# Where the third quarter's turns of layer 0's attention stand in the queues: step by step behind the first half's chain instead of behind the router

## The chip, the cores and the metric

The kernel runs on one core of a Trainium2 chip. A core has a matrix engine (PE), a vector engine (DVE), an engine for activation functions (ACT), a general engine (POOL), and a queue engine that starts transfers (SP). Each works through its own instructions in order; they wait for each other by semaphores. The metric is device time in microseconds (us): the median of three runs, which before the change is 1929.3 (1927.78 to 1932.83).

## The reference

An activation x of 4 rows, 1024 steps and 128 features goes through four layers. Each layer has a mixing part ("attn") and a part by token ("ffn"), and after each part a layer norm of the sum: x = norm(x + part(x)). What matters here are layers 0 and 1:

```python
# layer 0, attn: a short convolution gives a value, a gate and a score; then, for M = 4 angles,
phi = x5 * theta
re_m = poly * cos(phi);  im_m = poly * sin(phi)
num_re, num_im, den = split(cumsum(concat([p_w * re_m, p_w * im_m, p_w]), axis=1))
re = num_re / max(den, 1e-4);  im = num_im / max(den, 1e-4)
rs = rsqrt(mean of the squares over one head + 1e-5)
y = re * rs * norm_scale[:16] @ W_re + im * rs * norm_scale[16:] @ W_im
out = (y * silu(gate)) @ out_proj_w
# layer 0, ffn: x in blocks of 32 rounded to a 6 bit grid, times a weight treated likewise, plus a bias
# layer 1, attn: a complex recurrence h_t = a * h_{t-1} + B u_t; y_t = Re(C h_t)
# layer 1, ffn: a router picks 4 of 16 experts for each token; their outputs are added with weights
```

Both attention parts run along the steps, so a quarter of the steps needs the carried sums of the quarter ahead of it. The router and the experts go token by token.

## The kernel before, in words

The 1024 steps are cut into four quarters of 256. A tile of a quarter has 128 partitions (features) and 4 rows x 256 steps, so 1024 elements. The first two quarters are the first half, "a": they go ahead through layer 0 and layer 1 up to layer 1's experts, and the third and fourth follow beside that.

**Layer 0's attention** is `l0_attn` (L378 on). For each quarter, `prepare(q)` projects value, gate and score (16 matmuls of 512 columns and 16 of 256), and makes the weight `pq` and the running sum `den`. Then come four *turns*, one for each angle m. A turn takes, on ACT, two rows for `k` (L447, L448), then sine, Abs and sine again (L451, L452, L454); on DVE one row for `k` (L449), and for each of the parts im and re a product with `pq` (L456), the carry from the quarter before (L366) and a scan over the steps (`l0_scan`, L367); then on ACT a square of the scan's result (L460) and a copy of its last step (L369), and on PE two matmuls into `yv` and four for the sum of squares. The *close* of a quarter (L473 to L489) takes the root of that sum (L474, L475), spreads it over the heads on PE, scales the gate, projects, adds to x and normalizes (`norm`, L189 on: statistics on DVE at L196 and L197, the root on ACT at L200, an offset on DVE at L208, eight normalizing rows on ACT at L211).

**The first half's chain** goes on with `l0_ffn` (L530 on; quantizing rows on DVE, L499 to L519, into `xd`; the add to x is L563), `l1_attn` (L648 on; products at L669, scans at L673, carries at L683 to L689, a product on POOL at L691, the add to x at L700), and `l1_route`: logits on PE, a sigmoid on ACT (L785), then only DVE rows from L787 until it has written, at L1302, the positions at which each token's row goes into the lists of its experts. `spread` (L1373 on) then starts 64 indirect DMAs on POOL (L1327), one for 128 tokens and one of their four choices. The experts' first inputs are loaded by SP when all 64 have landed (`gathered`, L1392).

**What sets the order.** The kernel's functions are generators: each `yield (t,)` ends a step and gives its length as planned by hand. `run` takes a generator to its end. `mix(main, side, pace, drain)` alternates: after each step of the main one it takes steps of the side one until their lengths times `pace` make up for it. Each instruction of a side step gets a dependency, without a semaphore, on the last main instruction on its engine ("queued behind"). Then a scheduler orders each engine's instructions by times that it assumes and by these dependencies; in what is not bound by them it may draw an instruction forward past others. So the order in which the functions are called is not yet the order in a queue. `press(side, ready)` takes steps of a side generator until a condition holds.

Before the change, `all` runs `l0_attn((0, 1))`, which also prepares the third quarter, then the chain, the router, and after it `l0_attn((2, 3))` mixed with the spread:

```python
self.run(self.l0_attn((0, 1)))
...
self.run(self.l0_ffn((0, 1)))
self.run(self.l1_attn((0, 1)))
self.run(self.l1_route(a))
self.run(self.mix(self.l0_attn((2, 3)), self.spread("l1", a, K1)))
```

Buffers that matter: the projections' `z` lie in a pool of two in PSUM ("l0z"), which `l0_attn` opens and closes itself; `ms`, the sum of squares, is one of two buffers of the pool `side`, which the router uses as well.

Of the kernel before, what the change touches and what calls it, by code (L numbers as in the profile page):

```python
# [20 lines left out]
P = 128  # L21
# [53 lines left out]
class Kernel:  # L75
# [302 lines left out]
    def l0_attn(self, qs):  # L378

        nc, tc, col = self.nc, self.tc, self.col
        ts, tt = nc.vector.tensor_scalar, nc.vector.tensor_tensor
        x, x0T, taps, cb = self.x, self.x0T, self.taps, self.col["conv_b"]
        with ExitStack() as ctx:
            bp, tp, psy = self.l0_bp, self.l0_tp, self.l0_psy
            psz = self.pool(ctx, "l0z", 2, space=PSUM)
            pss = self.side

            def prepare(q):  # L390
                z2 = self.tile(pss, [P, BLK], "s")[:, :TQ]
                for k in range(CK):
                    for b in range(B):
                        self.mm(
                            z2[32 * b : 32 * b + 32, :], taps[:, k, 2 * P :], x0T[:, q, b, k : k + TQ],
                            k == 0, k == CK - 1,
                        )
                pw = self.tile(bp, [P, TQ], "pw")
                ts(pw, z2, cb[:, 2:3], col["score"], ALU.add, ALU.mult)
                ts(pw, pw, -20.0, 20.0, ALU.max, ALU.min)  # L400
                nc.scalar.activation(pw, pw, AF.Exp)
                tt(pw, pw, self.tw[:, q, :], ALU.mult)

                def project(ch):
                    z = self.tile(psz, [P, QC], "z")
                    for h in range(2):
                        for k in range(CK):
                            self.mm(
                                z[:, h * BLK : (h + 1) * BLK].rearrange("p (b t) -> p b t", b=2),
                                taps[:, k, ch * P : (ch + 1) * P],  # L410
                                x0T[:, q, 2 * h : 2 * h + 2, k : k + TQ],
                                k == 0,
                                k == CK - 1,
                            )
                    return z

                z = project(0)
                xv = self.tile(bp, [P, QC], "xv")
                nc.scalar.activation(xv, z, AF.Identity, bias=cb[:, 0:1])
                z = project(1)  # L420
                gate = self.tile(bp, [P, QC], "gate")
                nc.scalar.activation(gate, z, AF.Silu, bias=cb[:, 1:2])
                pwx = self.l0_spread(psz, pw)

                pq = self.tile(bp, [P, QC], "pq")
                ts(pq, xv, self.nw2, self.dw[:, 1:2], ALU.mult, ALU.add)
                tt(pq, pq, xv, ALU.mult)
                nc.vector.scalar_tensor_tensor(pq, pq, self.dw[:, 0:1], pwx, ALU.add, ALU.mult)
                den = self.tile(bp, [P, QC], "den", bufs=1)
                self.l0_scan(den, pwx, 2 * MF, q)  # L430
                ts(den, den, 1e-4, None, ALU.max)
                nc.scalar.activation(den, den, AF.Square)
                return xv, gate, den, pq

            made = self.l0_made
            if not made:
                made[qs[0]] = prepare(qs[0])
                yield (20.0,)
            for q in qs:
                xv, gate, den, pq = made.pop(q)  # L440
                ms = self.tile(pss, [P, BLK], "s")[:, :TQ]
                self.l0_by_head(ms, self.headd, den, True, False)
                yv = self.tile(psy, [P, QC], "yv")
                for m in range(MF):

                    k = self.tile(tp, [P, QC], "k")
                    nc.scalar.activation(k, xv, AF.Identity, scale=self.turn[:, m : m + 1], bias=self.rnd)  # L447
                    nc.scalar.activation(k, k, AF.Identity, bias=self.drop)  # L448
                    nc.vector.scalar_tensor_tensor(k, xv, self.turn[:, m : m + 1], k, ALU.mult, ALU.subtract)  # L449
                    im = self.tile(tp, [P, QC], "im")  # L450
                    nc.scalar.activation(im, k, AF.Sin, scale=2.0 * PI_IN)  # L451
                    nc.scalar.activation(k, k, AF.Abs)  # L452
                    re = self.tile(tp, [P, QC], "re")
                    nc.scalar.activation(re, k, AF.Sin, scale=-2.0 * PI_IN, bias=self.halfpi)  # L454
                    for part, v in ((1, im), (0, re)):
                        tt(v, v, pq, ALU.mult)  # L456
                        s = self.tile(tp, [P, QC], "s", bufs=3)
                        self.l0_scan(s, v, 2 * m + part, q)
                        sq = self.tile(tp, [P, QC], "sq")
                        nc.scalar.activation(sq, s, AF.Square)  # L460
                        first, last = m == 0 and part == 1, m == MF - 1 and part == 0
                        for h in range(2):
                            c = slice(h * BLK, (h + 1) * BLK)
                            self.mm(yv[:, c], self.wbd[:, part * MF + m, :], s[:, c], first, last)
                        self.l0_by_head(ms, self.head, sq, False, last)
                        yield (5.0,)
                    if m == 0 and q + 1 in qs:
                        made[q + 1] = prepare(q + 1)
                        yield (10.0,)
                if q == 1:  # L470
                    self.l0_weight()
                    made[q + 1] = prepare(q + 1)
                rs = self.tile(bp, [P, TQ], "rs")  # L473
                nc.scalar.activation(rs, ms, AF.Sqrt, scale=1.0 / (2.0 * HC * MF))  # L474
                nc.vector.reciprocal(rs, rs)  # L475
                rsx = self.l0_spread(psz, rs)
                for g in range(2):
                    c = slice(g * BLK, (g + 1) * BLK)
                    tt(gate[:, c], rsx[:, c], gate[:, c], ALU.mult)
                    tt(gate[:, c], yv[:, c], gate[:, c], ALU.mult)  # L480
                for g in range(2):
                    po = self.tile(pss, [P, 4, D], "s")
                    for k in range(4):
                        t = g * 4 + k
                        self.mm(po[:, k, :], gate[:, t * P : (t + 1) * P], self.w_out)
                    t0 = q * QT + g * 4
                    tt(x[:, t0 : t0 + 4, :], po, x[:, t0 : t0 + 4, :], ALU.add)
                self.norm(self.quarter(q), by="act", on_act=True)
                yield (10.0,)  # L489
# [1399 lines left out]
    def at_once(self, gen):  # L1889

        for _ in gen:
            yield (0.0,)

    def served(self, gen, *others):

        others = list(others)
        while True:
            while others and others[0][0]():
                yield from others.pop(0)[1]
            got = next(gen, None)  # L1900
            if got is None and not others:
                return
            yield got or (1.0,)
# [53 lines left out]
    def all(self):  # L1957
# [4 lines left out]
        with ExitStack() as ctx:  # L1962
            lgp = self.pool(ctx, "l2lg")
            self.l2_lg = self.tile(lgp, [P, NT, E2], "lg")
            with ExitStack() as early:

                self.l0_setup(early)
                self.l2_wr = self.load(lgp, self.ins["l2_wr"])
                with ExitStack() as room:
                    self.l0_room(room)  # L1970
                    self.run(self.l0_attn((0, 1)))
                    self.l1_setup()
                    self.zero_lists("l1")
                    self.run(self.l0_ffn((0, 1)))
                    self.run(self.l1_attn((0, 1)))

                    self.run(self.l1_route(a))
                    self.run(self.mix(self.l0_attn((2, 3)), self.spread("l1", a, K1)))
                self.zero_lists("l2", "l3")
                with ExitStack() as c2:  # L1980
                    wall = self.l1_wall(c2)
                    yp = self.pool(c2, "l1ya", 5, right=True)
                    side = self.chain(self.l2_norms(), self.l0_ffn((2, 3), True), self.l1_attn((2, 3), True))
                    self.run(self.mix(self.chain(self.l1_shared(a, self.l1_sw), self.l1_experts(a, wall)), side, 2.0, False))
                    self.run(self.mix(self.abreast(self.l2_weights(), side), self.l1_close(a, yp)))
# [237 lines left out]
```

## Time and profile before

| | before |
|---|---|
| median of three runs | 1929.3 us |
| the profiled execution | 1937.33 us |
| its span in the profile | 1935.5 us |
| PE busy | 1541.5 us (80%) |
| DVE busy | 1199.2 us (62%) |
| ACT busy | 900.6 us (47%) |
| POOL busy | 690.3 us (36%) |

The profile is of one execution; its times in the text are us from the start of its span. L12 is line 12 of the kernel before. "Busy" leaves out waiting. An arrow in brackets tells what ended the idle time ahead of an instruction. An instruction is written with the tile that it writes, an arrow, and the tiles that it reads. The granted clock is the share of full speed that PE had. In the changed kernel the lines stand up to three further down in most places.

### The profile page before, as it was taken

The page shows a single profiled execution, that of the slowest core. Times are in us where ns is not written, and L with a number is a line of the kernel's source. Part 1 is how long each engine was busy: PE and PEld are TensorE (multiplying, and loading weights), DVE is VectorE, ACT ScalarE, POOL GpSimd, SP SyncE. Part 2 cuts the span into 40 slices and gives each one's busy share as a digit, 9 for nine tenths or more (in the row PEclk, how much of TensorE's full clock was granted, in tenths as well). Part 3 has the DMA queues.
Part 4 walks back from the last instruction along what each step waited for, and adds up shares of the span by engine and source line. Part 5 has one row for each costly group of instructions (what it writes and reads, how often), then busy time and mean ns, then how long its engine had stood idle before and what let it go on. Part 6 is the DMA issues. An engine that isn't in the chain of part 4 may idle for free. (4 is left out here: it accounts for less than half of the span.)

```text
span 1935.5 us, 27095 instructions
## 1 busy us (share of the span) xinstructions
PE 1541.5 (80%) x9025; PEld 920.8 (48%) x9025; DVE 1199.2 (62%) x3491; ACT 900.6 (47%) x1349; POOL 690.3 (36%) x670
## 2 busy tenths in 40 slices
PE   7885677597847887989977878798798998999850
PEld 3332433385423345856632232333355757768650
DVE  8998698465766664635564565546442446866383
ACT  5876265243324554423336756564532236644330
POOL 2000148604630660265443000030536430567775
PEclk9897688798978998999988988898988999989985
DMA  9990002244430113632241000000452213425452
GB/s 297 288 288 10 1 17 86 87 126 133 159 129 18 60 63 129 183 96 73 78 137 32 1 1 1 2 23 1 159 213 83 66 28 93 141 68 167 122 147 61
DMA packets 215530, 187.10 MB, mean 97 GB/s; under 512 B 16528, under 2 KB 194064, under 8 KB 214864
## 3 DMA queue, kind: packets, MB, share of 16 engines
q1 hardware_dynamic: 194672, 142.29, 23.6%
q0 software_dynamic: 20704, 42.86, 7.3%
q8 instruction: 84, 1.38, 0.3%
q14 instruction: 70, 0.57, 0.1%
HBM read 88.49 MB, written 96.60 MB: 96 GB/s over the span
## 5 line engine op out<-in xcount | busy, mean ns | idle before, releaser
L1081 ACT ACTIVATE pr<-sc 128x1024 f32<-128x1024 f32 x288 | 279.4, 1021 | 175.2 <-PE sc L161 174.8
L161 PE MATMUL sc<-qm,kT 32*128 32x512 f32 (+3 forms) x1536 | 197.7, 559 | 16.7 <-ACT pr L1081 16.7
L161 PE MATMUL s<-pr,va 128*32 128x512 f32 (+3 forms) x1536 | 167.5, 532 | 19.0 <-DVE x L1019 10.2
L161 PE MATMUL gu<-ld,xgT 128*128 x640 | 165.1, 400 | 10.2 <-DVE hg L1812 5.9
L1087 DVE TENSOR_TENSOR pr<-pr,ld 128x512 f32<-128x512 f32 (+1 forms) x160 | 91.7, 581 | 105.6 <-ACT pr L1081 105.4
L161 PE MATMUL gu<-wall,xgT 128*128 x304 | 148.2, 612 | 2.0 <-ACT xgT L171 2.0
L161 PEld LDWEIGHTS sc<-qm,kT 32*128 32x128 f32 x1536 | 83.7, 194 | 112.4 <-issue 61.1
L161 PEld LDWEIGHTS gu<-ld,xgT 128*128 128x128 f32 x640 | 119.5, 198 | 34.7 <-DVE hg L1812 6.1
L1812 DVE TENSOR_TENSOR hg<-sg,gu 128x256 f32<-128x256 f32 x160 | 66.0, 417 | 92.0 <-ACT sg L1811 91.6
L173 DVE COPY hT<-tp 128x512 f32<-128x512 f32 x118 | 80.9, 686 | 66.2 <-PE tp L169 66.2
L1567 ACT ACTIVATE sg<-gu 128x512 f32<-128x512 f32 x76 | 45.4, 597 | 144.7 <-PE gu L161 143.6
L1811 ACT ACTIVATE sg<-gu 128x256 f32<-128x256 f32 x160 | 61.3, 385 | 107.7 <-PE gu L161 79.8
L171 ACT COPY xgT<-tp 128x512 f32<-128x512 f32 x99 | 58.0, 586 | 99.9 <-PE tp L169 99.8
L1327 POOL DMA_INDIRECT l1ra<-x,posl1a x64 | 79.8, 1246 | 61.3 <-DVE peq L1321 42.0
L1327 POOL DMA_INDIRECT l1rr<-x,posl1r x64 | 65.4, 1022 | 100.9 <-DVE posl1r L1302 70.8
L169 PEld LDWEIGHTS tp<-ld,hg 128*128 128x128 f32 x624 | 77.4, 141 | 49.0 <-issue 32.5
L1569 DVE TENSOR_TENSOR hg<-sg,gu 128x512 f32<-128x512 f32 x76 | 51.8, 682 | 78.9 <-ACT sg L1567 78.8
L1327 POOL DMA_INDIRECT l2rm<-x,posl2m x16 | 15.7, 983 | 236.8 <-DVE peq L1320 230.1
L169 PE MATMUL tp<-ld,hg 128*128 128x128 f32 x624 | 96.4, 275 | 3.7 <-DVE hg L1812 2.0
L1327 POOL DMA_INDIRECT l3ra<-x,posl3a x64 | 63.7, 996 | 93.3 <-DVE usedl3a L1315 51.0
L161 PEld LDWEIGHTS s<-pr,va 128*32 128x32 f32 x1536 | 37.1, 113 | 122.6 <-issue 78.4
L161 PE MATMUL yp<-ld,hT 128*128 x640 | 86.1, 276 | 2.3 <-DVE mv L197 1.5
(447 smaller groups left out, 3439.1 us busy)
## 6 DMA issues: line engine op xcount, KB each, us to landing
wall<-wall SPq DMA_DIRECT2D x16, 768.0 KB, 7.8
l3ra<-zero SPq DMA_DIRECT2D x1, 6144.0 KB, 25.5
ld<-in_l_w SPq DMA_DIRECT2D x2, 3072.0 KB, 10.6
wall<-we SPq DMA_DIRECT2D x24, 256.0 KB, 2.1
ld<-in_l_w SPq DMA_DIRECT2D x1, 6144.0 KB, 20.6
l1ra<-zero SPq DMA_DIRECT2D x1, 5120.0 KB, 19.6
l1rr<-zero SPq DMA_DIRECT2D x1, 5120.0 KB, 23.1
xg<-l3ra SPq DMA_DIRECT2D x20, 256.0 KB, 2.9
```

Of the source, the lines that this page charges most:

```text
L161: return self.nc.tensor.matmul(out, lhsT, rhs, start=start, stop=stop)
L169: nc.tensor.transpose(pt[:, k * P : (k + 1) * P], s, self.ident)
L171: nc.scalar.copy(dst, pt[:, : n * P])
L173: nc.vector.tensor_copy(dst, pt[:, : n * P])
L1081: nc.scalar.activation(pr, sc[h], AF.Exp)
L1087: nc.vector.tensor_tensor(d, d, cst["tril"].unsqueeze(1).unsqueeze(1).to_broadcast([P, 2, n, P]), ALU.mult)
L1327: ins = self.nc.gpsimd.indirect_dma_start(**kw)
L1567: nc.scalar.activation(sg, gu[:, 0, :], AF.Silu)
L1569: nc.vector.tensor_tensor(h, sg, gu[:, 1, :], ALU.mult)
L1811: nc.scalar.activation(sg, pg[:, :, 0, :], AF.Silu)
L1812: nc.vector.tensor_tensor(h[:, 2 * c : 2 * c + 2, :], sg, pg[:, :, 1, :], ALU.mult)
```

## The change

`l0_attn((2, 3))` is no longer called as a whole behind the router. Its first part, the four turns of the third quarter, is mixed into `l0_ffn` and `l1_attn` of the first half, eight steps of 5.0 at a pace of 2.7 against a chain of 108 planned units. Each step's instructions are queued behind the chain's latest on their engine. When all four turns are out, the generator notes "l0 turned" and is left where it is. Behind the router it goes on: the fourth quarter's preparation, the third's close, then the fourth quarter, mixed with the spread; here it is the main generator and the spread the side one, as before. The fourth quarter's preparation, which was written behind the third quarter's first turn, is now behind its last. The pool "l0z" is opened outside: once around the first two quarters, and again behind the router.

```diff
@@ l0_attn
-            psz = self.pool(ctx, "l0z", 2, space=PSUM)
...
-                    z = self.tile(psz, [P, QC], "z")
+                    z = self.tile(self.l0_psz, [P, QC], "z")
...
-                    if m == 0 and q + 1 in qs:
+                    if m == 0 and q != 2 and q + 1 in qs:
                         made[q + 1] = prepare(q + 1)
                         yield (10.0,)
                 if q == 1:
                     self.l0_weight()
+                if q == 2:
+                    self.listed.add("l0 turned")
+                    yield (0.1,)
+                if q in (1, 2):
                     made[q + 1] = prepare(q + 1)
...
+    def until(self, gen, ready):
+
+        while not ready() and (got := next(gen, None)):
+            yield got
@@ all
-                    self.run(self.l0_attn((0, 1)))
+                    with ExitStack() as z:
+                        self.l0_psz = self.pool(z, "l0z", 2, space=PSUM)
+                        self.run(self.l0_attn((0, 1)))
                     self.l1_setup()
                     self.zero_lists("l1")
-                    self.run(self.l0_ffn((0, 1)))
-                    self.run(self.l1_attn((0, 1)))
-
+                    more = self.l0_attn((2, 3))
+                    turned = lambda: "l0 turned" in self.listed
+                    self.run(self.mix(
+                        self.chain(self.l0_ffn((0, 1)), self.l1_attn((0, 1))), self.until(more, turned), 2.7, False
+                    ))
                     self.run(self.l1_route(a))
-                    self.run(self.mix(self.l0_attn((2, 3)), self.spread("l1", a, K1)))
+                    self.press(more, turned)
+                    self.l0_psz = self.pool(room, "l0z", 2, space=PSUM)
+                    self.run(self.mix(more, self.spread("l1", a, K1)))
```

More of the change, by code (lines that the diff above doesn't have):

```diff
@@ L422, in prepare @@
                 nc.scalar.activation(gate, z, AF.Silu, bias=cb[:, 1:2])
-                pwx = self.l0_spread(psz, pw)
+                pwx = self.l0_spread(self.l0_psz, pw)
                 pq = self.tile(bp, [P, QC], "pq")
@@ L475, in l0_attn @@
                 nc.vector.reciprocal(rs, rs)
-                rsx = self.l0_spread(psz, rs)
+                rsx = self.l0_spread(self.l0_psz, rs)
                 for g in range(2):
```

## The prediction, made before the changed kernel ran

> **What bounds the kernel at this place.** I read first the busy time of the engines in four stretches of the span (columns: length, busy us and instructions of PE, weight loads, DVE, ACT and POOL, granted clock, DMA share, GB/s), cut where the first half's chain changes its character.
>
> ```profile
> 140.00:194.35 54.35, 33.35 (x111) 17.92 (x112) 47.28 (x99) 33.39 (x57) 0.00 (x0) 0.78 0.13 37
> 194.35:242.01 47.66, 29.24 (x121) 22.03 (x121) 30.33 (x71) 10.75 (x24) 6.67 (x2) 0.68 0.00 1
> 242.01:265.71 23.70, 19.14 (x64) 8.24 (x66) 21.68 (x124) 12.13 (x11) 0.00 (x0) 0.86 0.00 1
> 265.71:364.69 98.98, 69.10 (x336) 35.12 (x328) 70.38 (x117) 54.98 (x71) 79.77 (x64) 0.86 0.21 78
> ```
>
> They are the quantized layer, layer 1's scan, the router, and the spread of the first half's rows (64 indirect DMAs on POOL). No engine is full in all four, so the bound is a chain. Second, POOL in order of time (start, duration, instruction, idle before it):
>
> ```profile
> 265.71 1.12 POOL L1327 DMA_INDIRECT l1ra<-x,posl1a  x1 [42.05 <-DVE peq L1321]
> 267.14 1.97 POOL L1327 DMA_INDIRECT l1ra<-x,posl1a  x1 [0.31 <-issue]
> 269.42 2.18 POOL L1327 DMA_INDIRECT l1ra<-x,posl1a  x1 [0.30 <-issue]
> 271.90 3.53 POOL L1327 DMA_INDIRECT l1ra<-x,posl1a  x1 [0.30 <-issue]
> ...
> 323.31 0.96 POOL L1327 DMA_INDIRECT l1ra<-x,posl1a  x1 [0.30 <-issue]
> ...
> 363.73 0.96 POOL L1327 DMA_INDIRECT l1ra<-x,posl1a  x1 [0.30 <-issue]
> ```
>
> POOL waits for nothing from the first to the last. Undisturbed, one takes 0.96 and the next starts 0.30 later: 64 x 1.26 = 81 us; the spread took 99. Third, DVE in order of time around it:
>
> ```profile
> 266.04 2.28 DVE L367 TENSOR_TENSOR_SCAN s<-keep,re 128x1024 f32<-128x1024 f32 x1
> 268.55 2.28 DVE L367 TENSOR_TENSOR_SCAN s<-keep,im 128x1024 f32<-128x1024 f32 x1
> 272.38 2.28 DVE L367 TENSOR_TENSOR_SCAN s<-keep,re 128x1024 f32<-128x1024 f32 x1
> ...
> 349.55 0.35 DVE L502 RECIPROCAL qri<-qsc 128x32 f32<-128x32 f32 x1
> 366.67 0.69 DVE L508 TENSOR_SCALAR qt<-qt 128x1024 int32<-128x1024 int32 x1 [16.77 <-POOL qt L505]
> ```
>
> From 350 to 367 DVE has nothing to do, and PE idles 17.11 us before 370.76: the experts' inputs wait until all 64 DMAs have landed, and DVE waits for the POOL product queued behind the spread. So the end of the spread sets what follows, one for one. Its end is the start of the spread, which is when DVE writes the positions (L1302), plus its length. The changed kernel must bring one of the two forward. Fourth, the first half's chain on DVE ahead of the router:
>
> ```profile
> 194.35 2.48 DVE L669 TENSOR_TENSOR b<-pu,wi 128x512 f32<-128x512 f32 x4 [5.85 <-PE pu L161]
> ...
> 209.69 0.69 DVE L700 TENSOR_TENSOR x<-po,x 128x512 f32<-128x512 f32 x1 [2.49 <-PE po L161]
> ...
> 227.53 0.69 DVE L700 TENSOR_TENSOR x<-po,x 128x512 f32<-128x512 f32 x1 [3.85 <-PE po L161]
> ...
> 242.01 0.42 DVE L787 TENSOR_TENSOR s<-sc,rows 128x256 f32<-128x256 f32 x1 [9.19 <-ACT sc L785]
> ```
>
> There are gaps to fill: with two smaller ones some 23 us. Which of the third quarter's work fills them already? None: between 194 and 265 DVE runs none of it. But of its four turns, all but three scans have run by 188, between the rows of the quantized layer.
>
> **What moves.** The written order says that the turns come behind the router; the scheduler had already drawn them forward. The instructions' order in the changed program, set against the old, shows on DVE: exactly three scans cross the router (2.28 us each, those of the third fence). On ACT six squares cross it, on PE the sums of squares and the last matmuls of three scans. The other moves are within the chain: turns 1 to 3, which stood in the quantized layer, now stand one by one in it, in layer 1's two quarters and just ahead of the router. POOL's and SP's queues keep their order; no DMA is added. The order of what follows the spread is the same. ACT gets two more loads of its function tables (98 against 96).
>
> So the price is how much of some 16 us of DVE work (two k rows at 1.2, four products at 1.15, four scans at 2.2, each from start to start) lies ahead of a chain row instead of in a gap. I walked the new order row by row, each row starting when its engine and its inputs are free, with the durations of the same rows of the trace. Four parts up to the router:
>
> 1. To layer 1's first scan: **-3.3**. Ahead of the first quantized tile (xd, L519) stood four scans, two k rows and three products, 14.9; now one scan, one product and one k row, 4.5. That is -10.4, less 1.3 for a product now ahead of the second quarter's close: -9.1. Behind it stood 4.6 of turns; now two products, two scans and a k row, 7.9: +3.3. A square (1.05) and a sine table swapped for the root's (1.28) stand ahead of the norm on ACT: with their waits +2.5.
> 2. To the root of layer 1's first norm: **+7.9**. A product and a scan stand ahead of the carry rows that release POOL's product (L691): +3.4. The second quarter's two scans now come ahead of the first add to x (L700), which waited for PE only 2.49: +3.6. A product and a scan stand ahead of the statistics, +3.3, and one scan of the chain no longer stands among them, -2.3.
> 3. To the root of the second norm: **+2.7**. The statistics are ready about as late as part 2 leaves them, but ACT is in turn 3: two k rows, sine table, two sines, one Abs, root table, some 8.2 in all, and ends 2.6 after them.
> 4. To the router's first row (L787): **+4.1**. A product and a scan stand ahead of the norm's offset, 3.4, of which 0.8 is covered by the wait for the root; a second scan and two squares break into ACT's eight normalizing rows, +2.2; the logits on PE, at a higher clock, -0.7.
>
> Sum +11.4. The gaps were waits of the chain for a round through ACT, PE or POOL, and in-order rows of 3.4 at their end push the round that follows. The router itself (23.7) keeps its rows: 0.
>
> **The spread: -3.8.** Its first four DMAs took 1.12 + 1.97 + 2.18 + 3.53 = 8.80, undisturbed 3.84: 4.96 too long. The second, third and fourth end 0.77 to 0.80 after a scan of the third fence ends. With the scans gone, the weights' products (L1320 and L1321, 0.42 each) and two k rows still stand there; I keep 1.2 for them. All the fourth quarter's scans and products stay in the spread. Bounds: 0, if these rows delay as much, and -4.96.
> The Trainium skill weighs in here: by "SBUF — State Buffer", section "Who interferes with whom", a DVE instruction with two SBUF inputs contends with GpSimd's reads alone, and it infers that descriptor generation needs the write interface, so that such rows don't stall a DMA. The rows above speak against that inference; by it the saving would be 0 and the sum +11.4.
>
> **PE's clock** in the new order isn't in the trace. In layer 1's stretch it was granted 0.68; 32 matmul records of L161 (po<-l1c,g) took 6.76 and 6.18, against 1.95 for 16 of po<-wT,xdT. The turns' matmuls between them may keep the clock up. The first product no longer decides (part 2); the second and the logits' second half (3.59) at full clock give -3.1 and -1.8 at most. Slower rows of this kind than these the trace doesn't have, so the other end is 0. I keep 0 to -4.9, and I take the -0.7 of part 4, nearer to the rows as they are.
>
> **Sum:** +11.4 - 3.8 = +7.6 us. Against the profiled execution (span 1935.5, time 1937.3) that is a span of 1943.1; against the median of the three runs, 1929.3, it is **1936.9**, +0.4%.
>
> **Rivals.**
> - *Slower still*: the spread keeps its length and turn 3 holds ACT for its full 8.2 behind the copies of xT. +11.4 and up to 3 more: 1941 to 1944. For it: each scan displaced is replaced by another of the fourth quarter sooner; against: those rows' count in the spread is unchanged. 0.10.
> - *No change*: half of parts 2 to 4 (14.7) falls into the gaps because rows end a little earlier than in my walk: +4 - 3.8 = 0, 1929. For it: 23 us of gaps; against: the scans stand directly ahead of the rows that wait. 0.18.
> - *Faster*: the gaps swallow the turns. PE's warmer clock brings the chain's rounds forward by 4.9, DVE's rows lie inside the waits, and of part 1's -3.3 most is kept; the router starts some 3 earlier and the spread is 3.8 shorter: -7, 1922. With a spread 3.8 shorter it turns to a gain where the positions (L1302), at 264.7 now, are written before 268.5, and to one of 0.3% before 262.7. 0.10.
> - *It does nothing*, as the scheduler had done it already. Three scans and the squares do move; counted with no change.
>
> **Chances.** The forecast has 0.62, with a range of its own of 1935.2 to 1941. What a measurement of this kernel can tell from no change is about 0.3%, 5.8 us. Slower by more: 0.62 + 0.10 = 0.72; within: 0.18; faster: 0.10. The range 1926 to 1944 leaves out most of the faster case and the end of the slowest; the costs' bounds (+11.4 with no saving; +11.4 - 4.96 - 4.2 = +2.2) lie inside.
>
> **What would show it.** Right: the first DMA of the spread starts near 277 instead of 265.71, the spread lasts about 95, no scan of the third quarter is left in it, and the experts' first row of DVE (L1812 before) comes some 8 later; on DVE, scans directly ahead of the statistics of layer 1. Wrong: the first DMA starts before 270, which breaks parts 2 to 4; a spread of 99 breaks the saving; a PE clock above 0.85 between the quantized layer and the router breaks the clock's term; another order of rows behind the spread, or a stage after it that changes its length, breaks "one for one".

## The result, and the profile after

The changed kernel takes **1944.2 us** (median of 8 runs, 1938.4 to 1945.5) against 1929.9 (8 runs, 1926.5 to 1935.6): a ratio of 1.0061, 95% interval 1.0046 to 1.0076, or +11.8 us (8.9 to 14.7); the medians themselves differ by 14.3. A ratio here and below is taken from the executions that lie within 1.5% of the fastest one of their kernel. The forecast was 1936.9, +7.6: the sign is right and the size too small; the median lies 0.2 over the end of the range of 1926 to 1944.

The profiled execution of the changed kernel has a span of 1939.1 and a time of 1941.13. That is only 3.8 over the profiled execution of before (1937.33). This execution of before was 6.8 slower than the mean of its 8 timed runs (1930.6), and that of after 1.6 faster than the mean of its own (1942.7); 3.8 + 6.8 + 1.6 makes the 12.2 between the means. So the two traces can be compared place by place, but their ends understate the loss.

First the engines' busy time in the four stretches, now cut at the changed kernel's own boundaries: its first row of layer 1's products, of the router, of the spread, and POOL's product behind the spread (columns as before: length, busy us and instructions of PE, weight loads, DVE, ACT and POOL, granted clock, DMA share, GB/s).

```profile
140.00:192.54 52.54, 35.41 (x144) 18.17 (x144) 39.20 (x88) 29.88 (x53) 0.00 (x0) 0.76 0.13 37
192.54:254.73 62.19, 38.24 (x171) 21.01 (x170) 47.67 (x86) 31.22 (x47) 6.67 (x2) 0.73 0.00 1
254.73:277.19 22.46, 16.43 (x62) 7.07 (x64) 21.63 (x124) 15.72 (x15) 0.00 (x1) 0.86 0.00 0
277.19:369.85 92.66, 63.34 (x252) 33.86 (x244) 62.42 (x113) 41.91 (x55) 73.44 (x64) 0.79 0.22 83
```

The lengths were 54.35, 47.66, 23.70 and 98.98. The quantized layer is 1.8 shorter and the router 1.2; the spread is 6.3 shorter; layer 1's scan is 14.5 longer, with 17.3 more on DVE and 20.5 more on ACT: the turns stand there now. PE's clock in it is 0.73, up from 0.68.

POOL in order of time, the start of the spread, its last DMA and the product behind it:

```profile
277.19 1.12 POOL L1330 DMA_INDIRECT l1ra<-x,posl1a  x1 [50.70 <-DVE peq L1324]
278.62 1.10 POOL L1330 DMA_INDIRECT l1ra<-x,posl1a  x1 [0.30 <-issue]
280.02 1.39 POOL L1330 DMA_INDIRECT l1ra<-x,posl1a  x1 [0.30 <-issue]
281.72 0.96 POOL L1330 DMA_INDIRECT l1ra<-x,posl1a  x1 [0.30 <-issue]
...
368.88 0.95 POOL L1330 DMA_INDIRECT l1ra<-x,posl1a  x1 [0.30 <-issue]
369.85 1.93 POOL L508 TENSOR_TENSOR qt<-x,qri 128x1024 f32<-128x1024 f32 x1
```

The first DMA starts 11.5 later than before (265.71), the first four take 4.57 instead of 8.80, and the product behind the spread, which stood at 364.71, starts 5.1 later. It follows the last DMA without a wait, as before.

DVE in order of time, at two places of the chain:

```profile
169.10 1.22 DVE L522 TENSOR_TENSOR xd<-qt,qsc 128x1024 f32<-128x1024 f32 x1
...
171.70 2.29 DVE L367 TENSOR_TENSOR_SCAN s<-keep,im 128x1024 f32<-128x1024 f32 x1
179.51 0.69 DVE L566 TENSOR_TENSOR x<-po,x 128x512 f32<-128x512 f32 x1 [5.53 <-PE po L161]
...
215.76 0.67 DVE L703 TENSOR_TENSOR x<-po,x 128x512 f32<-128x512 f32 x1
216.34 1.22 DVE L455 TENSOR_TENSOR re<-re,pq 128x1024 f32<-128x1024 f32 x1
217.47 0.69 DVE L703 TENSOR_TENSOR x<-po,x 128x512 f32<-128x512 f32 x1
...
218.14 0.29 DVE L196 BATCH_NORM_STATS2 bn<-x 128x6 f32<-128x128 f32 x1
218.35 2.28 DVE L367 TENSOR_TENSOR_SCAN s<-keep,re 128x1024 f32<-128x1024 f32 x1
```

The lower rows are what the forecast named: a product (L455) between the two adds to x (L703), and a scan behind the first row of the statistics. The upper rows are something that it did not name: the quantized tile xd starts at 169.10, and before the add to x DVE waits 5.53 for PE. PE in order of time says why:

```profile
170.47 1.94 PE L169 MATMUL tp<-ld,xd 128*128 128x128 f32 x8 [9.12 <-DVE xd L522]
172.24 1.23 PE L161 MATMUL po<-wT,xdT 128*128 128x128 f32 x4
174.04 3.78 PE L161 MATMUL yv<-s,wbd 128*128 128x512 f32 x4 [0.58 <-DVE s L367]
177.75 1.08 PE L161 MATMUL s<-sq,ld 128*32 128x256 f32 x8
178.76 1.60 PE L161 MATMUL po<-wT,xdT 128*128 128x128 f32 x12
```

The chain's sixteen matmuls into po are cut in two by the turn's matmuls, which had to wait for the turn's scan (171.70 to 173.99) and then took 3.78 and 1.08. In the kernel before, the sixteen run in one piece, and the add comes 5.8 behind xd (DVE and PE, two views of the same stretch):

```profile
177.65 1.20 DVE L519 TENSOR_TENSOR xd<-qt,qsc 128x1024 f32<-128x1024 f32 x1
183.44 1.28 DVE L563 TENSOR_TENSOR x<-po,x 128x512 f32<-128x512 f32 x2
```

```profile
180.75 1.95 PE L161 MATMUL po<-wT,xdT 128*128 128x128 f32 x16
```

ACT in the changed kernel, at turn 3 and the second norm:

```profile
238.44 1.15 ACT L453 ACTIVATE re<-k,halfpi 128x1024 f32<-128x1024 f32 x1
239.61 1.28 ACT L200 ACT_TABLE_LOAD   x1
240.90 0.30 ACT L200 ACTIVATE rstd<-mv,eps 128x8 f32<-128x8 f32 x1
```

The turn's last sine and the table load behind it end at 240.89 and set the root; DVE's last row of the statistics, itself behind a product of the turn, ends at 239.9.

### The profile page after: what moved, and what is told of

Read it like the earlier page. It is cut to its first block, busy times and chain, and to the rows that moved or that the text cites. A ratio compares the mean times of both kernels' runs of the same rounds, so it can differ in the third digit from the quotient of the medians.

```text
span 1939.1 us, 27097 instructions
## 1 busy us (share of the span) xinstructions
PE 1537.0 (79%) x9025; PEld 921.8 (48%) x9025; DVE 1200.9 (62%) x3491; ACT 902.9 (47%) x1351; POOL 689.9 (36%) x670
## 5 line engine op out<-in xcount | busy, mean ns | idle before, releaser
L161 PE MATMUL s<-pr,va 128*32 128x512 f32 (+3 forms) x1536 | 163.8, 522 | 20.5 <-DVE x L1022 9.7
L161 PE MATMUL yv<-s,wbd 128*128 128x512 f32 x128 | 77.6, 734 | 39.0 <-DVE s L367 35.6
L1330 POOL DMA_INDIRECT l1rr<-x,posl1r x64 | 65.9, 1030 | 100.0 <-DVE posl1r L1305 72.4
L1330 POOL DMA_INDIRECT l1ra<-x,posl1a x64 | 73.4, 1148 | 69.9 <-DVE peq L1324 50.7
## 6 DMA issues: line engine op xcount, KB each, us to landing
ld<-in_l_w SPq DMA_DIRECT2D x2, 3072.0 KB, 10.8
```

What stands on the lines that cost most here:

```text
L161: return self.nc.tensor.matmul(out, lhsT, rhs, start=start, stop=stop)
L1330: ins = self.nc.gpsimd.indirect_dma_start(**kw)
```

## The experiments

**Theories.** A: the turns cost what stands of them ahead of a row of the chain, the spread is long because DMAs wait for DVE rows, and its end hands the sum on. B: the loss comes from what was put behind the router (the third quarter's close, the fourth's preparation, the pool). C: a stage behind the spread has become longer by itself. D: DVE rows do not hold up the DMAs.

**The chips.** The twelve runs were made on three other chips of the same kind, on which the kernel before takes 2240 to 2244 us instead of 1930. The start and the end of the spread agree with the first trace (the kernel before starts it at 265.60 instead of 265.71 and ends it at 364.46 instead of 364.69), so they can be carried over; rows ahead of it differ between traces of one kernel by up to 3 us (layer 1's first scan stands at 196.75 and 198.69). The one repeated trace of before is from the first of the three chips, and places of all twelve are set against it. From 335 on the third and fourth quarters' own chain differs, and behind the spread everything does: the stretches of over 2 us in which PE, DVE and ACT all stand still come to 161 us in the kernel before, against 34 in the first trace. Times are compared only with runs of before on the same chip. They vary by 2 to 3% there, so most intervals are near 1% wide, and a ratio depends on which executions it is taken from: by the medians of all executions the two runs of psum_scan are 0.2% and 0.7% slower than before instead of the 1.4% and 1.0% in the table, in_ffn 0.7% instead of 0.0%, held_back 2.2% and held_psum 2.6%.

All runs in one table; us from the trace, the ratio against before with its 95% interval. "End" is the end of the last of the 64 DMAs, "product" the start of POOL's row behind it.

| kernel | first DMA | length | end | product | ratio |
|---|---|---|---|---|---|
| before, first trace | 265.71 | 98.97 | 364.69 | 364.71 | |
| after, first trace | 277.19 | 92.65 | 369.83 | 369.85 | 1.0061 (1.0046 to 1.0076) |
| before_again | 265.60 | 98.86 | 364.46 | 381.50 | one execution |
| after_again | 276.42 | 92.73 | 369.15 | 386.00 | one execution |
| after_second | 276.48 | 93.93 | 370.41 | 388.07 | 1.0024 (0.9981 to 1.0067) |
| pools_only | 264.87 | 97.36 | 362.24 | 377.88 | 1.0011 (0.9972 to 1.0050) |
| pools_only_second | 265.62 | 98.50 | 364.12 | 381.00 | 1.0018 (0.9981 to 1.0055) |
| in_ffn | 273.38 | 93.60 | 366.98 | 384.99 | 1.0004 (0.9962 to 1.0046) |
| psum_scan | 263.63 | 89.84 | 353.47 | 392.02 | 1.0143 (1.0075 to 1.0211) |
| psum_scan_second | 265.09 | 87.69 | 352.78 | 404.52 | 1.0099 (1.0056 to 1.0143) |
| psum_scan_after | 277.52 | 85.79 | 363.31 | 378.19 | 1.0081 (1.0036 to 1.0126) |
| psum_scan_after_second | 276.49 | 85.84 | 362.33 | 385.58 | 1.0003 (0.9946 to 1.0059) |
| held_back | 246.04 | 94.17 | 340.21 | 442.66 | 1.0180 (1.0091 to 1.0268) |
| held_psum | 246.30 | 86.08 | 332.37 | 447.04 | 1.0357 (1.0293 to 1.0421) |

**1. Both kernels again** (no edit).

> The kernel before, unchanged, for a second profile. Theory A (the change's price is the rows of the turns that stand ahead of rows of the first half's chain; the end of the spread sets what follows one for one): the first DMA of the spread starts within 1 us of 265.71 and the POOL product behind the spread within 1 us of 364.71, as in the first profile; what differs between two executions of one kernel lies behind 1100. Theory C (the stages behind the spread differ between the two kernels, beyond what the spread hands on): the stages behind 1100 lie within 1.5 us of those of the first profile.

> The changed kernel, unchanged, for a second profile. Theory A: first DMA within 1 us of 277.19, POOL product behind the spread within 1 us of 369.85, and behind 1100 an offset to the kernel before that differs from the first pair's (+5.9 at 1108, +0.9 at 1384) by as much as two profiles of one kernel do. Theory C: a stage behind the spread is longer than before by some 6 us in this profile too, at the place where it is in the timed runs.

> The changed kernel again, with a profile and five rounds, because the first repeat ran on a chip on which the kernel before takes 2240 us: there PE stands still in many places with no wait that the trace names, and POOL's product behind the spread waits for the other half's quantization instead of following the spread. Theory A: on a chip where the kernel before takes about 1930, the product follows the spread at once, at 369 to 370, and the time is 5 to 12 us over the kernel before. Theory C (a stage behind the spread is longer too): the stages behind 400 lie 10 us or more behind those of the kernel before.

The start and the end of the spread come again within 0.8 us in all three. The product at 369 to 370 does not: on these chips it waits, and what was expected for the stages behind 1100 can't be read on them. The kernel before, all engines in order of time around the end of the spread (rows left out between):

```profile
350.64 1.24 PE L161 MATMUL pg<-xT,ld 128*128 128x512 f32 x2
...
351.07 3.17 ACT L211 ACTIVATE x<-x,off,rstd 128x128 f32<-128x128 f32 x8
...
369.56 0.69 DVE L848 TENSOR_TENSOR x<-py,x 128x512 f32<-128x512 f32 x1 [23.51 <-remote]
369.64 0.60 ACT L763 ACTIVATE sg<-pg 128x512 f32<-128x512 f32 x1 [15.40 <-remote]
```

and POOL alone, a little later:

```profile
363.50 0.96 POOL L1327 DMA_INDIRECT l1ra<-x,posl1a  x1 [0.30 <-issue]
381.50 1.91 POOL L505 TENSOR_TENSOR qt<-x,qri 128x1024 f32<-128x1024 f32 x1 [17.04 <-DVE qri L502]
```

"remote" marks a wait that no recorded instruction or DMA ended. The third and fourth quarter's own chain stands still from 354 to 369, its quantization (qri) comes at 381 instead of 349.9, and so that chain, not the spread, releases POOL. The experts' first load does not follow the spread there either. In SP's queue it stands behind the reading of a flag that the other half's chain writes (DVE at L897, read at L2040), and in all twelve traces it goes out 6 to 7 us behind that reading (376.35 and 382.70 in before_again); in the first trace of before the flag is read at 345.07 and the load goes out at 366.14, behind the last DMA. C is neither shown nor excluded: against before_again, after_again is mostly 4 to 8 late up to 900, 22 at 1030 and 24 at its end; after_second ends 14 late; but pools_only_second, whose spread ends within 0.4 us of before_again's, is 17 late at 1030 and 23 at its end. Offsets there vary between executions and chips by more than the effect.

**2. The change without its mixing.** The chain runs plainly; pools, close and preparation stay as changed.

```diff
-                    self.run(self.mix(
-                        self.chain(self.l0_ffn((0, 1)), self.l1_attn((0, 1))), self.until(more, turned), 2.7, False
-                    ))
+                    self.run(self.l0_ffn((0, 1)))
+                    self.run(self.l1_attn((0, 1)))
                     self.run(self.l1_route(a))
-                    self.press(more, turned)
```

> The changed kernel with the chain run plainly, as before: the turns are not mixed into it; the pool for z opened outside, the fourth quarter's preparation behind the third's last turn, and the close behind it stay as changed. Theory A (the loss is the turns ahead of chain rows): first DMA at 265.7 within 1 us, spread of 98 to 99, time within 3 us of the kernel before, 1927 to 1932. Theory B (the loss is what was moved behind the router: the fourth quarter's preparation and the third's close, beside the spread): the spread's end stays 5 us late or more, and the time 8 us or more over the kernel before.

> The change without the mixing of the turns into the chain, again. Theory A: first DMA at 265 within 1 us, spread's end 361 to 365, the time within 0.2% of the kernel before or up to 3 us under it. Theory B (the loss is what was moved behind the router): 5 us or more over it.

First DMA at 264.9 and 265.6, end 2.2 and 0.3 sooner than before_again's. All of the 11 us at the start of the spread come from the mixing, and B is refuted up to the spread's end. The two ratios agree with no change; less than 0.5% they could not have shown, so for the time B is only unlikely.

**3. All four turns mixed into the quantized layer.**

```diff
-                    self.run(self.mix(
-                        self.chain(self.l0_ffn((0, 1)), self.l1_attn((0, 1))), self.until(more, turned), 2.7, False
-                    ))
-                    self.run(self.l1_route(a))
+                    self.run(self.mix(self.l0_ffn((0, 1)), self.until(more, turned), 1.4, False))
                     self.press(more, turned)
+                    self.run(self.l1_attn((0, 1)))
+                    self.run(self.l1_route(a))
```

> The changed kernel with all four turns mixed into the quantized layer alone; layer 1's two quarters are run plainly behind it. Theory A: the turns cost where they stand ahead of the chain's next row, wherever that is; first DMA 8 to 12 us later than before, the spread 5 to 6 us shorter, its end 3 to 7 us later, time 1934 to 1940. A rival (the loss is in layer 1's part alone, where the statistics wait behind scans, parts 2 to 4 of the sum): the first DMA within 2 us of 265.7, its end some 5 us sooner than before, time 1922 to 1926.

Against before_again, layer 1's first scan is 8.4 late, the two roots 8.1 and 7.9, the router's first row 7.9, the first DMA 7.8: the whole loss arises in the quantized layer and layer 1 hands it on unchanged. In the changed kernel on the same chip the same places stand at -2.6, +4.8, +7.9, +11.7 and +10.8. So the price goes where the turns go, as A says (its numbers for first DMA and end, 8 to 12 and 3 to 7, are just missed from below, at 7.8 and 2.5), and the rival (layer 1 alone) falls. The time does not tell the versions apart.

**4. The products in PSUM.** Theory A's second half: the DMAs wait for DVE rows with two inputs in SBUF. The fourth quarter's product is written to a PSUM tile, so the scan has one input there; no row is added.

```diff
-                        tt(v, v, pq, ALU.mult)
+                        p = self.tile(psz, [P, QC], "z") if q == 3 else v
+                        tt(p, v, pq, ALU.mult)
...
-                        self.l0_scan(s, v, 2 * m + part, q)
+                        self.l0_scan(s, p, 2 * m + part, q)
```

> The kernel before, with one edit: in the fourth quarter the product goes to a tile in PSUM, so that the scan behind it has one input in SBUF instead of two (the order of the instructions stays). Theory A (POOL's indirect DMAs wait for DVE rows with two SBUF inputs, and the spread's end sets what follows): first DMA at 265.7 to 266, the DMAs beside these scans take 0.96, the spread is some 5 to 7 us shorter, and the POOL product behind it comes 5 to 7 us sooner than 364.71; the time falls by as much where the stages behind keep their length. Rival D (such rows do not hold up the descriptors; the DMAs are long for another reason): spread of 98 to 99, nothing gained.

> The kernel before with the fourth quarter's products in PSUM, again. The first run ended the spread at 353.5, 11 us sooner than the kernel before on the same sort of chip, but the product behind it waited for the other half's quantization (qri). On a chip where the kernel before takes about 1930, qri is written at 349.55 and 15 us of slack are there. Theory A: the product follows the spread at 355 to 358, time 5 to 9 us under the kernel before. Rival (the other half's chain binds as soon as the spread is shorter): the product waits for qri, time as before.

> The changed kernel with the same edit (the fourth quarter's scans take the product from PSUM). Theory A: first DMA at 277 as in the changed kernel, spread some 6 us shorter than its 92.7, so the spread's end within 2 us of the kernel before (364 to 366): the time as before within 2 us, on the same chip. Rival D: spread 92 to 93, time as the changed kernel's, some 5 us over the kernel before.

> The changed kernel with the fourth quarter's products in PSUM, again. In the first run the spread's end lay 1.1 us ahead of the kernel before's although it began 11.9 later. Theory A: product behind the spread at 363 to 366, time within 3 us of the kernel before, so that the changed kernel's loss is gone. Rival (the loss sits behind the spread): time as the changed kernel's.

D falls. In the first trace of before a scan of the fourth quarter stands beside a DMA like this (DVE and POOL, two views):

```profile
304.09 2.29 DVE L367 TENSOR_TENSOR_SCAN s<-keep,re 128x1024 f32<-128x1024 f32 x1 [0.99 <-PE yv L161]
```

```profile
304.14 3.01 POOL L1327 DMA_INDIRECT l1ra<-x,posl1a  x1 [0.30 <-issue]
```

In psum_scan such a scan takes as long as before, and the DMAs beside it have their undisturbed length (two views of the same 3 us):

```profile
301.80 2.29 DVE L367 TENSOR_TENSOR_SCAN s<-keep,z 128x1024 f32<-128x1024 f32 x1
304.09 2.24 DVE L367 TENSOR_TENSOR_SCAN s<-keep,z 128x1024 f32<-128x1024 f32 x1
```

```profile
301.62 0.96 POOL L1328 DMA_INDIRECT l1ra<-x,posl1a  x1 [0.31 <-issue]
302.88 0.96 POOL L1328 DMA_INDIRECT l1ra<-x,posl1a  x1 [0.30 <-issue]
304.14 0.95 POOL L1328 DMA_INDIRECT l1ra<-x,posl1a  x1 [0.30 <-issue]
```

All 16 DMAs that begin beside a scan with an input in PSUM take 0.95 to 0.96 in psum_scan, while the third quarter's three scans, which still have both inputs in SBUF there, hold up three DMAs to 1.97, 2.18 and 3.52. With both inputs in SBUF such a scan made the DMA that it held up 1.8 to 3.5 long. The order did not stay as was expected (some rows of DVE and ACT behind the router stand in another), but POOL's did, and the lengths beside the scans do not rest on it.

The Trainium skill's page "SBUF — State Buffer", section "Who interferes with whom", infers that a DVE instruction with two SBUF inputs does not stall descriptor generation. By these runs it does hold up an indirect DMA (1.8 to 3.5 against 0.96). Each of these DMAs also takes its positions from a tile (`posl1a`, L1301), and no run separates the reading of positions from the making of descriptors: which of the two waits is not shown.

What the 64 DMAs take over 0.96 each falls from 18.2 to 9.2 and 7.1, in the changed kernel from 12.1 to 5.1 and 5.2. The spread is 9 us shorter than before's in psum_scan, more than the 5 to 7 expected; it is 11 shorter in psum_scan_second, but there the fourth quarter ran so late that three of its eight scans lie behind the spread. In the changed kernel it is 7 shorter: its end then lies at 362 to 363, ahead of before's 364.5, although it begins 11 to 12 later. The time does not follow. The product waits for qri in all four runs, and in the kernel before with this edit it comes 10 and 23 us later than without. Whether the edit delays that chain or the chips do is not shown: in both runs it stands still in the fourth quarter (PE, DVE and ACT together for 13 us from 318.6 in psum_scan), at waits that no record ends, and with the same edit in the changed kernel the product comes 8 and 0.4 us sooner than in after_again. What the edit does to the time on the first chip, where 14.8 us of slack lie between qri and the product, was not measured.

**5. The opposite of the change.** The turns are queued behind the router's last instruction on each engine, so that the scheduler can draw none forward; in the second version the third and fourth quarters' products also go to PSUM.

```diff
@@ the change without its mixing
+    def behind(self, gen):
+        while got := self.queued(gen):
+            yield got
...
+                    n = len(self.traced)
                     self.run(self.l1_route(a))
+                    self.latest.update((i.engine, i.name) for i in self.traced[n:])
...
-                    self.run(self.mix(more, self.spread("l1", a, K1)))
+                    self.run(self.mix(self.behind(more), self.spread("l1", a, K1)))
```

> The opposite of the change: the third quarter's turns are queued behind the router's last instruction on each engine, so that no turn stands in the first half's chain, not even those that the scheduler draws forward into the quantized layer in the kernel before. Theory A: the chain loses the rows of the turns (10.4 in the quantized layer alone, and the three scans behind it do not matter): first DMA 15 to 20 us sooner than 265.7, the spread 2 to 5 us longer as all of the quarter's scans then lie in it, its end 11 to 17 us sooner. A rival (the spread's end is not what sets the time: the third quarter's own chain ends last, so that the turns must be early): first DMA as soon as that, but the experts' first inputs and the third quarter's add to x come no sooner, time as before or longer.

> The turns queued behind the router, and the product of the third and fourth quarters in PSUM. Theory A: both gains add: first DMA 15 to 20 us sooner than 265.7 and a spread of 90 to 96, its end 18 to 24 us sooner than before. If the third quarter's own chain decides instead, nothing more than in the run without the PSUM product.

The chain without any turns reaches layer 1's first scan at 183.2 and the first DMA at 246.0; the kernel before has them at 198.7 and 265.6 (the scan at 196.8 in its first trace). So the turns that the kernel before has in the quantized layer cost 14 to 15.5 us there, and the rows beside the router another 4. A's number for the start is met. The spread was to be 2 to 5 us longer and is 4.7 shorter (with PSUM 12.8): the turns come so late that 8 of their scans lie beside it instead of 11, so its end is 24 and 32 us sooner, more than the 11 to 17 and 18 to 24 expected. The time is longer by 1.8% and 3.6%, and the rival's reason stands in POOL's and in SP's order of time (held_back, two views):

```profile
339.25 0.96 POOL L1330 DMA_INDIRECT l1ra<-x,posl1a  x1 [0.30 <-issue]
442.66 1.91 POOL L508 TENSOR_TENSOR qt<-x,qri 128x1024 f32<-128x1024 f32 x1 [102.45 <-DVE qri L505]
```

```profile
443.85 13.63 SPq L1395 DMA_DIRECT2D xg<-l1ra  x5
```

POOL then waits 102 us (115 in held_psum) for the third and fourth quarter's quantization, whose turns now all lie behind the router. The experts' first load goes out 104 us behind the spread's end, since SP reads the other half's flag at 437.80. Bringing the spread forward pays only as far as the other half's chain has slack.

None of these versions beats both kernels.

## Why the prediction was right, and where not

**The four parts up to the router.** Predicted against measured, from the same places of two pairs of traces:

| part | predicted | first pair | again, one chip |
|---|---|---|---|
| 1, to layer 1's first scan | -3.3 | -0.1 | -2.6 |
| 2, to the first root | +7.9 | +6.2 | +7.4 |
| 3, to the second root | +2.7 | +2.7 | +3.1 |
| 4, to the router's first row | +4.1 | +3.9 | +3.8 |
| the router | 0 | -1.2 | -0.9 |
| sum: first DMA | +11.4 | +11.5 | +10.8 |

The sum is right; in the first pair partly by luck, since part 1 was 3.2 dearer than forecast and part 2 and the router 1.7 and 1.2 cheaper. On the one chip no part is off by more than 0.9. Part 1's own first step held: -9.1 was forecast to the first quantized tile (xd), and it came 8.6 sooner (9.5 on the one chip). What was left out behind it is PE's queue. The working counted DVE's and ACT's rows behind xd and let PE hide its own; in the trace the turn's yv and sums matmuls stand ahead of twelve of the chain's po, and xd to the add to x took 10.4 instead of 5.8 (10.2 instead of 6.2 on the one chip). That is 4.6 of the gain of 8.6 gone in one place. A part of what the sum had priced behind xd lies under that wait, so the error that is left in part 1 is smaller: +5.8 forecast behind xd, +8.4 measured (+6.9). At the first root, parts 1 and 2 together came to +6.1 (+4.8) against +4.6.

Part 3's number is right by another sum: ACT ended 1.0 behind the statistics, not 2.6, and the statistics themselves fell 1.8 further behind, with a k row and a product of the turn among them. The router's 1.2 is a wait of DVE for ACT that it had before (1.18 ahead of the row at 251.17) and has no longer.

**PE's clock.** In layer 1's stretch it is 0.73 against 0.68, under the 0.85 that was to break the term. The rows that the term named became shorter by more than the 0.7 that was taken and less than the bound of 4.9: the second group of 32 (po<-l1c,g) took 5.12 instead of 6.18, the logits' second half 1.96 instead of 3.59. The add to x behind the first of these still waits 7.21 for po, against 3.85.

**The spread: mis-sized.** Predicted -3.8, bounds 0 and -4.96, measured -6.3. That the scans hold up the DMAs is shown by the PSUM runs. The first four DMAs gave 4.2 of it (0.7 of delay is left, for which 1.2 was kept). The other 2.1 is outside the bounds that were set: they took the fourth quarter's scans as unchanged in number, hence in cost. Their number is unchanged (8), but the cost of one depends on how it meets a DMA: the longest behind the first four was 3.01 before, where a scan began with the DMA (304.09 and 304.14), and is 2.62 now. A bound by count was no bound.

**One for one.** At the spread's end the sum was +7.6 and is +5.1; by this the time should have been nearer to no change, and it is +11.8. With the spread's term right the forecast would have been +5.1, so that +7.6 lies nearer to the time is luck. The product does follow the spread at once in the first pair, and the stages behind keep about +5 to +7 until 1100; then the pair comes together to +0.9 at 1384 and ends at +3.6. So the step that failed is "the sum is made against the profile's own time and added to the median": one profile of each kernel does not tell what the medians differ by. Where the other 4 to 10 us of the timed difference arise **stays open**. The second traces do not settle it, as offsets there change by 20 us between executions that agree at the spread's end.

**The rivals.** *Slower still* gave 1941 to 1944, near the time, but by another way: it had the spread keep its length and turn 3 hold ACT 3 us more, and neither happened (6.3 shorter; part 3 at +2.7). *No change* and *faster* asked for the turns to fall into the gaps; the first DMA at 277 excludes both. That the change *does nothing* is excluded by pools_only, which is 11 us apart from it at that row.

## What to carry to other kernels

Side work queued step by step behind a chain costs by every in-order queue that it enters: walk PE's order as carefully as DVE's, since a matmul that waits for a side scan holds the chain's matmuls behind it. Before paying to bring forward a transfer, look for the next arrival at the same consumer: here POOL's product waited for the other half's quantization, and SP's load for its flag, as soon as these were late. A delay by contention between two queues depends on how their rows meet, so bound it by the worst overlap times the count, not by the rows seen in one place.

## What the runs showed of the hardware that was not expected

- A scan on DVE with one input in PSUM takes the same time (2.29) as with both in SBUF, and leaves indirect DMAs beside it at 0.96; with both in SBUF the DMA that it holds up takes 1.8 to 3.5. The first trace of before has the same contrast: beside `den`'s scan, whose input is in PSUM, a DMA took 0.95 (281.60). Products with both inputs in SBUF delay too: one of 1.22 that began with a DMA made it 2.03 (psum_scan, 290.39).
- Chips of one kind differ. The same kernel takes 1930 and 2240 us. The busy time of DVE, ACT and POOL agrees within 1% (DVE 1199.2 and 1198.3), PE's is 4% longer at a lower granted clock (0.85 against 0.90), and the rows start within 3 us of each other up to 335. Then, in the kernel before at 352 to 370, PE runs nothing while DVE and ACT wait for what PE had been writing, with no releaser in the trace; POOL's DMAs go on beside it at 0.96. The count of matmuls is the same in both traces (9025), so none is missing in one alone. The cause was not found.
